# A planner's account of transfers and fillers, and the constants of its order, changed

## The chip, the cores and the metric

One core of a Trainium2 chip runs the whole program. The core has a matrix engine (TensorE, PE in the profile, with its weight loads shown apart as PEld) and three engines that work on 128 partitions side by side: VectorE (DVE), ScalarE (ACT) and GpSimd (POOL). SyncE (SP) issues the transfers. Each engine works through its own queue in order and waits at an instruction until what it needs is there. The metric is the device time of one execution in microseconds (us), as the median of some runs.

## The reference

Eight sequences of 512 rows and 128 channels pass through four layers, each of them added to its input. `ln` is a layer norm without scale.

```python
x = x + mamba(ln(x))       # W_in, short convolution, Silu, a scan over the 512 rows with 8 states
x = x + experts(ln(x))     # all 8 experts, dense, weighted by a router
x = x + attention(ln(x))   # 16 heads of 8 channels, each row sees its chunk of 10 and 25 rows before it
x = x + experts(ln(x))     # the same weights again
```

```python
g = einsum('bsh,ehf->ebsf', x, w_gate)
u = einsum('bsh,ehf->ebsf', x, w_up)
h = silu(g) * u
expert_out = einsum('ebsf,efh->ebsh', h, w_down)
out = einsum('ebsh,bse->bsh', expert_out, cw)    # cw from two softmaxes
```

The experts are most of the arithmetic: 8 experts of 128 x 512 up, 128 x 512 gate and 512 x 128 down, for 4096 rows, twice.

## The kernel before

**How the work is tiled.** A sequence's 512 rows are the columns of a tile, its 128 channels the partitions. A product of 32-bit precision is made of three passes in a rounded format (`matmul3`: high x high, low x high, high x low). So each operand is kept as a high half (a cast, mostly on ScalarE) and a low half (a subtraction, mostly on GpSimd). For one expert and one quarter of its 512 inner columns there are three products each into `g`, `u` and `y`, of 512 columns; between `u` and `y` stand Silu of `g` (ScalarE), its product with `u` (VectorE), the cast to the high half (ScalarE or VectorE) and the low half (GpSimd or VectorE). In the profile all four steps have `h` as their result. The weights are split into halves the same way as they arrive.

**What runs beside what.** The expert products of both expert layers form one stream (`ffn_stream`): layer k (0 or 1), sequence b (0 to 7), expert, quarter. Everything else is a set of generators, called lanes, that are woven into it: for each sequence a Mamba front (norm, `tp_m`, `mh`, convolution, `mde`, and the exponentials and logarithms of `mdelta`), a Mamba back (four times: `mbx`, decays `mdec`, scan `mst`, `mcc`; then `mo`), the norm and router ahead of the experts (`ffn_prep`: `tp_f`, the logits `lps_f`, `rps_f`, a softmax `pr_f`, `cps_f`), the weights of the router spread over the partitions by a transfer (`cwb`), the end of a sequence's experts (`yp`), and the attention's preparation, loads, scores (`as`), maxima (`amt`), weights (`aw`), values (`ao`) and output (`aout`).

**What sets the order.** The order of every engine's queue is fixed when the program is built, by a planner in the kernel file. `Clock` keeps an account of when each engine is free and what each operation costs (`cost`); `Engine` records every operation through one line, L269, which is why nearly all rows of the profile have that line. `Lanes.tick` chooses the lane that can start earliest; `Lanes.start` says when one can:

- Work of the experts' own chain is urgent (`hurry`) and may start up to `EDGE` early; sequence 0's first half goes with `FIRST`, its second half with `SECOND`.
- A lane whose next step is on TensorE joins the stream when its inputs have been there for `SIDE` plus a slack of `JOIN` (or the lane's own `JOIN_MAX` for the attention's maxima, `JOIN_ATT` for its preparation, `JOIN_END` for the end of the experts and of attention).
- A lane that is due is preferred by `PRESS`, and its slack is `JOIN_DUE`. Mamba is due `MAMBA_DUE` of a sequence's expert work ahead of its turn, the norm ahead of the experts `PREP_DUE`.
- While the stream itself waits, other work is held back by `HELD`.
- The softmax of the router waits until ScalarE's exponential table is loaded anyway, or until `LATE` of a sequence before it is needed.

**The first sequence** is done in two halves of 256 rows, so that the experts can begin early: `first_halves` for Mamba, then the first `SPLIT` experts on the first half, the same experts on the second half, and the rest on the whole (`passes`).

**Products of nothing.** TensorE's clock is kept up by products whose results are thrown away. Before the first expert product the planner places one (`warm`) whenever no lane can go on; its cost is that of a 256-column product plus a fixed step. Later, up to `WARM_TO` sequences, it places one (`idle`) when the stream has waited for `WARM_GAP` by the account (`keep_warm`).

**Transfers** are all issued by SyncE. In `Clock.run` the account of one is: queued behind the transfers before it, a fixed delay, its bytes at 200 KB per us, and a delay until the data can be read.

Of the kernel before, what the change touches and what calls it, by code (L numbers as in the profile page):

```python
# [87 lines left out]

TABLES = {AF.Silu: (18,), AF.Exp: (0, 6), AF.Ln: (6,), AF.Tanh: (0, 18)}
INF = float("inf")  # L90
LAGS = {"T": 0.2, "A": 0.15, "V": 0.15, "P": 0.08}
TO_PE = 0.11
SAME = 0.125
AHEAD = 0.2
EDGE = 0.1
FIRST = 0.6
LATE = 0.3
SIDE = 0.5
JOIN = 2.0
JOIN_DUE = 0.0  # L100
JOIN_MAX = 6.0
JOIN_ATT = 3.0
JOIN_END = 2.0
MOST = 6
OTHERS = 4
AT_FIRST = 7
WARM = 3.5
WARM_GAP = 0.25
WARM_TO = 1.5
SECOND = 0.2  # L110
PRESS = 0.4
HELD = 0.18
MAMBA_DUE = 0.9
PREP_DUE = 0.9
ATT_LEAD = 2.5
EARLY = 5
SPLIT = 4
EARLIEST = 2 * (DEPTH + 1)


def size(ap):

    n = 1
    for d in ap.shape[1:]:
        n *= d
    return n


class Clock:
# [96 lines left out]
    def based(self, key, base=None):  # L226
# [4 lines left out]
            [other + lag if other else 0.0]  # L231
            + [t + (LAGS[k] + lag if k != key else SAME if k in "AVP" else 0.0) for k, t in ends.items()]
        )

    def run(self, key, name, out, args, kw, after, wait):
        c = self.cost(key, name, out, args, kw)
        start = max(self.end[key] + wait, after, self.now if key == "T" else self.based(key))
        if key == "T":
            if start > self.end["T"] + 2.4:
                self.cold = start  # L240
            if start < self.cold + 3.4:
                c *= 2
        if key in "VP" and self.shares(key, name, out, args):
            start = self.with_port(start, c)
        self.end[key] = start + c
        if key == "S":
            start = max(start, self.now)
            row = out.shape[-1]
            rows = out.shape[0] * size(out) // row
            each = max(row * (2 if out.dtype == BF16 else 4), 512)  # L250
            move = rows * each / 200e3
            self.moved = max(self.moved, start + c + 0.8) + move
            return self.moved + 0.6 + move
        self.hop[key] = start + c
        return start + c + LAGS[key]

# [23 lines left out]
class Lanes:  # L280
# [29 lines left out]
    def add(self, gen, rank=1, ready=0.0, due=None, joins=None):  # L310


        self.lanes.append([gen, "", ({}, ready), rank, due, JOIN if joins is None else joins])
        self.lanes.sort(key=lambda lane: lane[3])
# [5 lines left out]
    def start(self, lane):  # L320
# [3 lines left out]
        if callable(need):  # L324
            return 0.0 if need() else INF
        if need == "T":
            if lane in self.urgent:
                return c.now if c.based("T", ready) <= c.now else INF
            wait = SIDE
            if not c.beside and not self.starved:  # L330
                wait += JOIN_DUE if lane[4] and lane[4]() else lane[5]
            return c.now if c.based("T", ready) + wait <= c.now else INF
        return min((max(c.end[key], c.based(key, ready)) for key in need), default=0.0)

    def tick(self):
# [3 lines left out]
        while True:  # L339
            c.now = max(c.now, c.end["T"])  # L340
            first, best = c.now + AHEAD, None
            for lanes in (self.urgent, self.lanes):
                for lane in lanes:
# [3 lines left out]
                    else:  # L347
                        edge = PRESS if lane[4] and lane[4]() else 0.0
                        if self.starved:
# [28 lines left out]
def block_kernel(ctx: ExitStack, tc: tile.TileContext, x, pack_a, pack_b, pack_c, w_qkv, mask, mask_t, w_o,  # L378
                 w_gate, w_up, w_down, out):
    nc = tc.nc  # L380
    clock = Clock()
# [66 lines left out]
    def load_x(b, i, tag):  # L448

        yield from lanes.take("x")  # L450
        if i:
            yield "S", done[b, i]
        t = lnp.tile([P, NT, DIM], F32, tag="x", name=f"x_{tag}", bufs=NX)
        e = sp.dma_start(out=t, in_=xs[b, i].rearrange("(t p) d -> p t d", p=P))
        return t, e
# [6 lines left out]
    def now(gen):  # L462

        try:
            next(gen)
        except StopIteration as stop:
            return stop.value
        raise AssertionError("no buffer is free")
# [30 lines left out]
    def layernorm(xc, tag, nt=NT, quick=False):  # L499
# [22 lines left out]
        for t in range(nt):  # L522
            yield "V" if quick else "AV"
            a = INF if quick else max(clock.end["A"], clock.based("A")) + 0.39
            v = max(clock.end["V"], clock.based("V")) + 0.255
# [109 lines left out]
    first = lambda gen: lanes.hurry(gen, FIRST)  # L635
    second = lambda gen: lanes.hurry(gen, SECOND)

    def mamba_front(b, sb, consts, xc):
# [25 lines left out]
        act.activation(xb[0:INNER, :], v[0:INNER, :], AF.Silu)  # L664
        there = clock.end["A"] + LAGS["A"]
        act.activation(xb[INNER:P, :], v[0:INNER, :], AF.Silu)
        there2 = clock.end["A"] + LAGS["A"]
        yield "T", there2
# [29 lines left out]
        act.activation(delta, delta, AF.Ln, bias=1.0)  # L698
        handed[b] = xb, zb, delta, bc, bc_there, clock.end["A"] + LAGS["A"]

# [322 lines left out]
    def ffn_prep(k, b, xc, t0=0, nt=NT):  # L1023
# [42 lines left out]

        yield lambda: clock.table in TABLES[AF.Exp] or pos[0] >= k * B + b - LATE
        yield "A"
# [44 lines left out]
    def ffn_finish(k, b, acc):  # L1113
        xo, there = yield from load_x(b, 2 * k + 1, f"fo{k}_{b}")
        yield "T", there
        tp = yield from side([P, NT, DIM], f"yp{k}_{b}")
        for t in range(NT):
            pe.transpose(tp[:, t, :], acc[:, t * P : (t + 1) * P], ident)
        yield "V"
        freed(dve.tensor_tensor(xo, xo, tp, ALU.add))  # L1120
        yield "S"
        store_x(b, 2 * k + 2, xo)

    def ffn_stream():
# [6 lines left out]
        def passes(k, b):  # L1131

            whole = slice(0, L)
            if k or b:
                return [(e, whole) for e in range(NE)]
            parts = [(e, slice(c * HALF, c * HALF + HALF)) for c in range(2) for e in range(SPLIT)]
            return parts + [(e, whole) for e in range(SPLIT, NE)]

        def weighted(k, b, e, cs, y, there):
# [25 lines left out]
            elif left[0] == 0:  # L1165
                lanes.add(ffn_finish(k, b, state.pop(("acc", k, b))), rank=FRANK, ready=t, joins=JOIN_END)

# [255 lines left out]
    def attention(sb):  # L1423
# [21 lines left out]
        def places(v):  # L1445
            return v.rearrange("p (i c) -> p i c", i=4)[:, :, :P].rearrange("p i (j c) -> p i j c", j=4)
# [25 lines left out]
        def load_values(s):  # L1472
# [10 lines left out]
            dve.tensor_copy(places(vtiles[s % 2])[:nk, :, :, :HD], vr[:nk])  # L1483
            v_there[s] = clock.end["V"] + LAGS["V"]

        def scores(s, both):

            qs, ks, _ = loaded[s]
            for m in range(NPAIR):
                for h in range(2):  # L1490
                    rows = slice(64 * h, 64 * h + QROWS)
                    for i, (q, k) in enumerate(blocks(steps[s][1])):
# [4 lines left out]
                        )  # L1497
            lanes.add(maxima(s, both, e), joins=JOIN_MAX)

# [101 lines left out]
        def outputs(s, o, e):  # L1601
# [11 lines left out]
            if t == len(QTILES) - 1:  # L1613
                lanes.add(joined(b, outs.pop(b)), rank=JRANK, ready=e, joins=JOIN_END)

# [103 lines left out]
    with mctx:  # L1719
        sb = msb  # L1720
        mc = {}

        def late(part):
            return lambda: pos[0] >= turn[part] - MAMBA_DUE

        def fronts(seqs):
            for b in seqs:
                turn["front"] = b
                xc = first_x
                if b:  # L1730
                    xc = yield from load_x(b, 0, f"m{b}")
                    yield lambda: ("front", b - 1) in done
                yield from mamba_front(b, sb, mc, xc)
                done["front", b] = 0.0

        def backs(seqs):
            for b in seqs:
                turn["back"] = b
                yield lambda: b in handed and (b - 1, 1) in done
                yield from mamba_back(b, sb, mc, lambda gen: lanes.add(gen, due=late("back")))  # L1740

        first(fronts(range(1)))
        first(mamba_consts(sb, mc))
        lanes.add(ffn_weights(sb))
        clock.hold = INF

        warm = now(side([P, L], "warm"))
        while (0, 0) not in ready or ready[0, 0][1] == 0:
            if lanes.tick():
                continue  # L1750
            if clock.now > WARM:
                sel = mc["sel"]
                e = pe.matmul(warm[:, :HALF], sel[:, 0], sel[:, : HALF // P], start=True, stop=True)
                clock.end["T"] += 0.1
            else:
                clock.now += 0.03
        freed(e)

        done["first"] = 0.0
        lanes.add(backs(range(1, B)), due=late("back"))  # L1760
        lanes.add(fronts(range(1, B)), due=late("front"))
        lanes.add(ffn_preps(), rank=0, due=lambda: pos[0] >= turn["prep"] - PREP_DUE)
        lanes.add(attention_preps(), rank=QRANK, joins=JOIN_ATT)
        stream = ffn_stream()

        def keep_warm():

            if pos[0] < WARM_TO and clock.now > clock.end["T"] + WARM_GAP and lanes.are_free("bank"):
                t, = take("experts", [[P, L]], ["idle"])
                sel = mc["sel"]  # L1770
                freed(pe.matmul(t[:, :HALF], sel[:, 0], sel[:, : HALF // P], start=True, stop=True), "experts")

        while "weights" not in done or (B - 1, 1) not in done:
            if next(stream):
                lanes.idle()
                keep_warm()
            else:
                lanes.tick()
# [85 lines left out]
```

## Time and profile before

| what | value |
|---|---|
| time, median of 3 runs | 1352.26 us (1350.01 to 1354.05) |
| the profiled execution | 1351.71 us, span 1349.9 us, granted TensorE clock 0.996 |
| TensorE busy | 1328.8 us, 98% of the span |
| products into u, g, y | 451.4, 448.4 and 445.6 us busy |
| GpSimd, low halves of h | 492 of 1309 ns |
| ScalarE, Silu of g and casts of h | 512 of 597 ns, 437 of 618 ns |
| VectorE, h from u | 420 of 686 ns |
| ScalarE, table loads | 125 (109 and 16 by line) of 1283 ns |

The busy times of the three kinds of expert products overlap a little, since one product begins before the one before it has left the array. The page's slices show TensorE at nine tenths or more in all but the first and the last of 40, and the chain of work that ended last lies on TensorE for 91% of the span. What the page alone doesn't show is how much of the busy time is work: fillers and products that wait inside a run are busy too.

### The profile page before, as it was taken

Reading aid. Unit: us, or ns where it says so; the run is one execution under the profiler, and the core shown is the slowest. Engines: PE = TensorE matmul, PEld = TensorE weight load, DVE = VectorE, ACT = ScalarE, POOL = GpSimd, SP = SyncE. Lnnn points to the kernel's source line nnn. Section 1 sums busy time; section 2 is a strip of 40 time slices with the busy share of each in tenths; the row PEclk is TensorE's granted clock in tenths of the full one; section 3 lists DMA queues with packets and bytes.
Section 4 is the critical chain, followed back from the end, with each engine's and each line's share of the span. In section 5 each row is a group of like instructions: output and inputs, shape, how many; then the busy total and the mean of one; then the engine's idle time right before and its main releaser. Section 6 shows DMA issues by size and latency. Waiting matters only on the chain.

```text
span 1349.9 us, 29483 instructions
## 1 busy us (share of the span) xinstructions
PE 1328.8 (98%) x10261; PEld 1053.4 (78%) x10261; DVE 1038.5 (77%) x3114; ACT 964.2 (71%) x1694; POOL 941.4 (70%) x1042
## 2 busy tenths in 40 slices
PE   7999999999999999999999999999999999999998
PEld 7877778788788877777777777777777777778886
DVE  6887888688888877897788887888888787845443
ACT  7768576867787556776777777777877767765654
POOL 5877576776767757676766767767677676777776
PEclk9999999999999999999999999999999999999999
DMA  4320303232111261344344453344443434121111
GB/s 126 95 82 28 87 24 101 64 80 76 42 48 56 63 86 52 72 102 113 79 102 114 98 125 88 95 110 102 104 99 96 114 76 102 47 71 53 40 40 40
DMA packets 182204, 107.74 MB, mean 80 GB/s; under 512 B 86401, under 2 KB 162088, under 8 KB 182056
## 3 DMA queue, kind: packets, MB, share of 16 engines
q1 hardware_dynamic: 182056, 105.87, 31.6%
q8 instruction: 81, 1.33, 0.4%
q14 instruction: 67, 0.55, 0.1%
HBM read 77.64 MB, written 27.79 MB: 78 GB/s over the span
## 4 chain that ended last, share of the span: by engine, by line
PE 91%; ACT 2%; issue 2%; POOL 2%; DVE 1%; POOLq 0%; DVEq 0%
PE u L269 26%; PE g L269 25%; PE y L269 25%; PE ao L269 2%; PE aw L269 2%; PE as L269 2%; PE mo L269 1%; POOL h L269 1%; PE aqk L269 1%; ACT h L269 1%; DVE h L269 1%; PE aout L269 1%; PE mde L269 1%; PE yp L269 1%; PE tp_f L269 0%
## 5 line engine op out<-in xcount | busy, mean ns | idle before, releaser
L269 POOL TENSOR_TENSOR h<-h,h 128x512 fp32r<-128x512 f32 x492 | 639.8, 1309 | 280.0 <-ACT h L269 223.2
L269 PE MATMUL u<-xt_f,wu 128*128 128x512 f32 (+1 forms) x1584 | 451.4, 395 | 3.6 <-ACT h L269 2.7
L269 PE MATMUL g<-xt_f,wg 128*128 128x512 f32 (+1 forms) x1584 | 448.4, 393 | 2.1 <-ACT h L269 1.9
L269 PE MATMUL y<-h,wd 128*128 128x512 f32 (+1 forms) x1584 | 445.6, 392 | 1.4 <-POOL h L269 0.8
L269 DVE TENSOR_TENSOR h<-u,h 128x512 f32<-128x512 f32 x420 | 285.8, 686 | 157.7 <-PE u L269 109.8
L269 ACT ACTIVATE h<-g 128x512 f32<-128x512 f32 x512 | 303.4, 597 | 124.8 <-PE g L269 100.6
L269 ACT CAST h<-h 128x512 fp32r<-128x512 f32 x437 | 268.3, 618 | 169.2 <-DVE h L269 167.6
L269 PEld LDWEIGHTS g<-xt_f,wg 128*128 128x128 f32 x1584 | 288.5, 189 | 70.2 <-ACT h L269 3.0
L269 PEld LDWEIGHTS y<-h,wd 128*128 128x128 f32 x1584 | 288.3, 188 | 70.3 <-POOL h L269 1.5
L269 PEld LDWEIGHTS u<-xt_f,wu 128*128 128x128 f32 x1584 | 286.7, 189 | 71.5 <-ACT h L269 4.1
L269 POOL TENSOR_TENSOR acc<-acc,cwb 128x512 f32<-128x512 f32 (+1 forms) x114 | 148.0, 1298 | 52.1 <-DVE cwb L269 44.9
L269 ACT ACT_TABLE_LOAD x109 | 139.8, 1283 | 25.2 <-PE g L269 23.7
L269 DVE CUSTOM_DVE_ANT_0 amasked<-as,maskq 128x60 f32<-128x60 f32 x640 | 95.3, 213 | 4.9 <-PE as L269 4.6
L269 DVE TENSOR_TENSOR cwb<-y,cwb 128x512 f32<-128x512 f32 (+1 forms) x116 | 77.4, 668 | 14.1 <-PE y L269 13.6
L269 DVE TENSOR_TENSOR apt<-aw,maskk 125x400 f32<-125x400 f32 (+2 forms) x160 | 88.1, 570 | 0.0
L269 DVE SCALAR_TENSOR_TENSOR h<-h,g 128x512 f32<-128x512 f32 x92 | 62.3, 681 | 28.3 <-ACT h L269 27.8
L269 ACT ACTIVATE apt<-apt 125x400 f32<-125x400 f32 (+2 forms) x160 | 81.5, 540 | 0.4
L269 DVE SCALAR_TENSOR_TENSOR h<-u,h 128x512 f32<-128x512 f32 x92 | 62.5, 683 | 3.3 <-PE g L269 0.5
L269 DVE DVE_READ_ACCUMULATOR2_ANT amx<- 128x1 f32 x640 | 51.9, 81 | 0.0
L269 DVE CAST h<-h 128x512 fp32r<-128x512 f32 x75 | 50.6, 675 | 1.2
L269 DVE COPY v<-avr 125x128 f32<-125x128 f32 (+2 forms) x40 | 25.5, 638 | 26.5 <-PE ao L269 26.0
L269 PEld LDWEIGHTS ao<-apt,v 125*32 125x32 f32 (+2 forms) x1280 | 27.4, 109 | 14.6 <-DVE h L269 4.0
(205 smaller groups left out, 1241.4 us busy)
## 6 DMA issues: line engine op xcount, KB each, us to landing
cwb<-cwd_f SPq DMA_DIRECT2D x124, 256.0 KB
aqd<-apc SPq DMA_DIRECT2D x32, 192.0 KB
ks<-aqd SPq DMA_DIRECT2D x48, 93.8 KB
x_fo<-x SPq DMA_DIRECT2D x16, 256.0 KB
aqd<-apc SPq DMA_DIRECT2D x32, 128.0 KB
x_f<-x SPq DMA_DIRECT2D x15, 256.0 KB
qs<-aqd SPq DMA_DIRECT2D x48, 75.0 KB
aod<-aos SPq DMA_DIRECT2D x24, 100.0 KB
```

The lines of the kernel that those rows point to most:

```text
L269: f(*args, **kw)
```

## The change

Two constants of the account of a transfer, the step of a filler (now named `FILL`), and the constants of the order. The code of the planner and of the computation is otherwise the same.

```diff
+FILL = 0.02
-LATE = 0.3
+LATE = 0.4
-JOIN = 2.0
+JOIN = 3.5
-JOIN_MAX = 6.0
+JOIN_MAX = 3.0
-JOIN_END = 2.0
+JOIN_END = 3.0
-WARM_GAP = 0.25
+WARM_GAP = 0.15
-SECOND = 0.2
-PRESS = 0.4
+SECOND = 0.1
+PRESS = 0.2
-MAMBA_DUE = 0.9
+MAMBA_DUE = 1.0
-SPLIT = 4
+SPLIT = 5
...
-            self.moved = max(self.moved, start + c + 0.8) + move
-            return self.moved + 0.6 + move
+            self.moved = max(self.moved, start + c + 0.6) + move
+            return self.moved + 0.8
...
                 e = pe.matmul(warm[:, :HALF], sel[:, 0], sel[:, : HALF // P], start=True, stop=True)
-                clock.end["T"] += 0.1
+                clock.end["T"] += FILL
```

Since the planner's account decides what comes next everywhere, the order of all engines' queues differs from the first filler on. The heads of TensorE's two queues (a number is how many in a row; the last numbers of a name are layer, sequence and part):

| | before | after |
|---|---|---|
| warm products up to the first `g`, in 13 runs | 111 | 161 |
| of these ahead of `mh`, of `tp_f`, of `lps_f` | 8, 23, 7 | 13, 33, 11 |
| idle products | 30 | 34 |
| experts done on the first half ahead of the second | 4 | 5 |
| table loads up to the first Silu of sequence 1, and of sequence 2 (layer 0) | 13, 19 | 7, 18 |
| table loads in all | 125 | 130 |

## The prediction

> **What bounds the kernel now.** I read the page first, then the engines' busy time by stage, then TensorE's timeline at the start, then ScalarE's in the stage where the largest late gap lies.
>
> ```profile
> PE 1328.8 (98%) x10261; PEld 1053.4 (78%) x10261; DVE 1038.5 (77%) x3114; ACT 964.2 (71%) x1694; POOL 941.4 (70%) x1042
> L269 PE MATMUL idle<-sel 128*128 128x256 f32 x30 | 8.9, 337 | 2.9 <-DVE cwt_f L269 0.9 <-ACT h L269 0.8 <-DVE mst L269 0.7
> core 0: us, PE busy (x) PEld busy (x) DVE busy (x) ACT busy (x) POOL busy (x), PEclk, DMA share, GB/s
> 34.25:59.10 24.85, 24.49 (x179) 21.64 (x179) 21.24 (x54) 16.22 (x31) 19.44 (x25) 1.00 0.32 91
> 59.10:119.30 60.20, 57.62 (x330) 47.39 (x329) 47.19 (x99) 47.53 (x85) 44.83 (x49) 0.97 0.25 72
> 119.30:213.10 93.80, 89.95 (x404) 70.39 (x403) 75.73 (x152) 65.72 (x112) 64.45 (x69) 0.98 0.18 51
> 213.10:293.90 80.80, 79.35 (x369) 63.36 (x368) 61.56 (x119) 60.08 (x102) 57.72 (x56) 1.00 0.30 82
> 293.90:371.90 78.00, 78.00 (x365) 62.11 (x364) 67.60 (x122) 58.08 (x102) 50.73 (x49) 1.00 0.22 62
> ```
>
> TensorE sets the end, but 98% busy is not 98% useful: filler products count as busy, and so do products that wait for an operand inside a run. So I count useful work instead: each product by its pace in an undisturbed run (three 512-column products in 0.70 us, six 256-column ones in 0.72, 0.11 for 128 columns), fillers at zero, and compare the sum with the clock on the wall. The expert products' places in the trace give the dates. At the first expert product (34.25 us) TensorE is 29.2 us behind its useful work; at the first product of sequence 0's second half (59.1) 36.4; where the router logits of sequence 1 are formed (118.1) 48.8; at the first product of sequence 1 (129.0) 51.1, of sequence 2 (213.1) 59.7, of sequence 3 (293.9) 64.1, of sequence 4 (371.9) 67.7. So 29 us go before the experts, 30.5 in the first two sequences, 8 in the next two. In the last stretch TensorE is busy through, and the last 80 us stand in both programs in the same order on the four compute engines. What can change is the first 300 us, where no other engine is full: VectorE's 75.73 of 93.80 is the most.
>
> ```profile
> 8.76 1.12 PE L269 MATMUL mh<-mxt,win 128*128 128x512 f32 x3
> 12.99 0.67 PE L269 MATMUL mbc<-mxb,wbc 64*128 64x256 f32 x2 [1.80 <-ACT mxb L269]
> 23.33 0.80 PE L269 MATMUL mbx<-mbc,sel 128*128 128x256 f32 x2 [2.57 <-DVE mst L269]
> 24.56 1.91 PE L269 MATMUL mo<-pa,mcx 128*128 128x128 f32 x8
> 27.54 1.05 PE L269 MATMUL mo<-pa,mcx 128*128 128x128 f32 x8
> 28.34 3.00 PE L269 MATMUL warm<-sel 128*128 128x256 f32 x23
> 31.77 0.50 PE L269 MATMUL tp_f<-ident,xn_f 128*128 128x128 f32 x2 [0.43 <-DVE xn_f L269]
> 20.00:30.00 10.00, 7.43 (x52) 7.22 (x51) 9.33 (x22) 9.28 (x20) 3.69 (x3) 0.83 0.00 0
> ```
>
> Ahead of the experts the latency of sequence 0's first half decides, and fillers (warm) sit in TensorE's queue between its steps. After the 2.57 us of idleness the granted clock falls to 0.83 over 20 to 30 us, and eight mo products take 1.91 us instead of 1.05.
>
> ```profile
> 164.71 1.28 ACT L569 ACT_TABLE_LOAD   x1
> 166.00 1.30 ACT L269 ACTIVATE mdelta<-mdelta 128x512 f32<-128x512 f32 x2
> 167.32 1.28 ACT L269 ACT_TABLE_LOAD   x1
> 168.61 1.09 ACT L269 ACTIVATE h<-g 128x512 f32<-128x512 f32 x2
> 169.72 1.28 ACT L569 ACT_TABLE_LOAD   x1
> 171.01 1.95 ACT L269 ACTIVATE mdec<-mdelta,nega 128x512 f32<-128x512 f32 x3
> 176.65 1.65 PE L269 MATMUL g<-xt_f,wg 128*128 128x512 f32 x3 [1.94 <-ACT h L269]
> ```
>
> A burst of a Mamba sequence: 11.3 us of ScalarE with four table loads and only two of the Silus (h from g) that the experts need. TensorE runs dry: 1.94 us of waiting, and products at half pace after it; 3.8 us are lost between 170 and 180 by the count above.
>
> **The change, part by part.** No kind of operation is new; the two programs differ in counts and order. Counts: 50 more warm and 4 more idle products; SPLIT makes 36 products of 512 columns into 72 of 256 (0.232 against 2 x 0.119: nothing); 5 more table loads; 5 casts, 2 weight halves and 2 reads of maxima go to VectorE, 4 halves to GpSimd; one broadcast transfer becomes two. By the rows' means that is +2.6 us on VectorE, +2.9 on ScalarE, +2.8 on GpSimd over the whole span, hidden under TensorE as long as they stay below the 84% that VectorE bears from 300 to 400 us with TensorE full.
>
> *First part, up to the first expert product.* FILL makes the build put a filler every 0.02 us of its account on top of a product's cost; a filler really steps 0.12. I walk the path. 25 fillers (23 before) ahead of tp_m and 13 (8) before mh: mh starts at 9.5 instead of 8.76, but ScalarE reads it only after its own copies end at 10.25, so 0.2 late. 10 (6) before mbx: 1.3 us into a wait of 1.1, 0.2 more; then 0.3 late. Of the 2.57 us of idleness, 14 more fillers of 0.12 in the three runs before it leave about 1.0. The 1.80 us at 12.99 left the clock at 1.00, the 2.57 did not, so I take it that 1.0 keeps it: eight mo products cost 0.9 for 1.9, the second mo no longer waits 0.8 us for TensorE, and ends 0.4 earlier. GpSimd's weight halves also end 0.7 earlier (one cast is moved ahead of the second half's decays). Then 33 fillers, 4.0 us, stand before tp_f where the data need 3.0: tp_f at 32.0 against 31.77. 11 (7) more before the logits give 0.5, the idle product ahead of the first expert product (0.42) is gone. Sum +0.2 us; if the clock drops all the same, mo pays 0.8 twice: +1.9; if the filler is covered everywhere, -0.1.
>
> The Trainium skill (TensorE: Matmul & The Clock Gate, What's actually happening) has the clock drop only after a whole idle window of some 3.4 us. Here 2.57 us were enough. By that rule the closer fillers would save nothing, and this part would be +1.0.
>
> *Second part, sequence 0 (SPLIT, MAMBA_DUE, PRESS, SECOND).* The fifth expert's half stands before the second half now, and sequence 1's Mamba back is spread behind more expert work. Useful work ahead of the second half: +4.1 us; ahead of sequence 1's logits: +8.2. What these two points wait for is the other queues. Work queued ahead of the same points: VectorE +2.3 and +3.6 (its part of the transposed input), ScalarE +2.9 and +0.8, GpSimd's variance step +3.8 and +5.3. If the queues keep the idle time they have, the point comes later by what stands in front of it, and TensorE has that much more to do meanwhile. At the logits: 8.2 - 3.6 = 4.6 won by VectorE, 2.9 by GpSimd, 7.4 by ScalarE. I take VectorE's, the fullest (47.19 and 21.24 us in the two stretches): -4.6; bounds -7.4 and 0.
>
> *Third part, sequences 1 and 2.* Sequence 2's Mamba front is put off by 20 to 30 us of TensorE work, so its burst lands behind sequence 1's first product: five table loads (5 x 1.283), softplus 1.3, decays 2.7, with two Silus, 11.6 us. That is the burst of 164.71 over again, 3.8 us; in its old place 100 to 120 us lost 2.1 and part of that stays, so +2.8. The next burst has a third Silu and casts in its middle: half of its 3.8 is left, -1.9 and 0.3 of rounding up its cover: -2.2. Sum +0.6. In all, 13 us of ScalarE and 9 of VectorE move into this stretch: 70 and 74 of some 84 us; bounds 0 and +6 (both bursts at full price with the half clock).
>
> The skill (ScalarE: Activation LUTs, What ACT_TABLE_LOAD costs) adds a drain of 1.38 us to each load. Here an ACTIVATE follows 0.01 us after it. With the drain the first burst would be 7 us longer, and this part some +5.
>
> *Fourth part, the rest.* JOIN 2.0 to 3.5 lets side products join only after more slack; JOIN_MAX cuts that of the maxima. TensorE passes between 128-row products and the narrower ones 105 times in and out instead of 108: 3 x (0.09 + 0.14) = 0.7 us saved, as the gap at each edge is in the trace. The gaps of 1.6 us at 263 and 0.9 at 521 can go or double. I take -1.0; bounds -3 and +3.
>
> *Transfers.* The account lands a 256 KB load 2.7 us after its issue instead of 4.0; in the trace the first x is issued at 0.72 and read at 3.71. No engine but SyncE waited over 1 us for a transfer after the start, so earlier reads cost nothing while landings stay near 3 us; this works only through the order, in the parts above.
>
> Sum: +0.2 - 4.6 + 0.6 - 1.0 = -4.8 us. The profiled execution took 1351.71 (span 1349.9), 0.55 below the median of 1352.26; from the median: **1347.5**.
>
> **Rivals.** *The sides wash out* (no change): GpSimd's 3.8 us ahead of the second half against 4.1 of TensorE leaves 0.3, and the rest of the second part is lost in sequence 1 again, since the same work stands ahead of sequence 2's first product in both programs (useful work differs by 0.9, VectorE's by 1.8). For it: that equality. Against: 30 us of loss with no full engine. About 1352. *The ramp empties* (more): sequence 0's 20 us of loss halve, since up to its expert 7 ScalarE has 14.7 us less in front (six table loads fewer by sequence 1's first product) and VectorE 8.3: 1351.7 - 10 - 1 = about 1341. *ScalarE's burst* (slower): it stands between sequence 1's first and fourth Silu; with PSUM banks held by products of g, TensorE stops after some 6 us. If the burst of sequence 3 behaves so too, 3.8 + 3.8 us plus two half-clock windows of 1.7, against no more than 4 us won before: +7, 1359. It decides once sequences 1 and 2 lose over 8.7 us more than now. *Fillers in the way* (the change undoes itself): +1.9 in the first part and nothing won: 1354 to 1357.
>
> **Numbers.** Forecast 0.40, ramp 0.12, wash-out 0.26, burst 0.18, fillers 0.04. 0.3% is 4.1 us, about what a measurement of this kernel tells from no change: faster (below 1348.2) 0.52, same 0.26, slower (above 1356.3) 0.22. The forecast's own range is 1343 to 1349.5; with 2 in 10 left out, 1340 to 1357.
>
> **What would show it.** After: first expert product at 34.5 +- 0.7; no low clock near 25 us, and none of the 1.91 us mo; the second half's first product near 61.5 and sequence 1's near 124 instead of 129; behind useful work at sequence 1 some 46, at sequence 2 some 56. Wrong, if tp_f comes after 33, if sequence 1 starts after 129, or if a gap over 3 us follows the table loads behind its first products.

## The result and the profile after

The changed kernel takes 1361.76 us (median of 6 runs, 1359.99 to 1363.81), the kernel before 1351.61 beside it (6 runs, 1350.01 to 1354.05): 1.0076 times as long, 95% interval 1.0062 to 1.0089. The span of the profiled execution went from 1349.9 to 1359.7 us.

The page's line of busy times:

```profile
PE 1334.8 (98%) x10351; PEld 1060.4 (78%) x10351; DVE 1044.1 (77%) x3122; ACT 965.1 (71%) x1688; POOL 942.5 (69%) x1045
```

The group of the idle products (count, busy, mean ns, idle time before them and what ended it):

```profile
L270 PE MATMUL idle<-sel 128*128 128x256 f32 x34 | 10.2, 353 | 9.1 <-ACT h L270 3.8 <-DVE mst L270 2.0 <-DVE xt_f L270 1.3
```

The engines' busy time by stage (from the first expert product to the second half, to sequence 1's first product, and to those of sequences 2, 3 and 4):

```profile
core 0: us, PE busy (x) PEld busy (x) DVE busy (x) ACT busy (x) POOL busy (x), PEclk, DMA share, GB/s
35.25:69.30 34.05, 29.97 (x219) 27.17 (x217) 28.27 (x60) 20.91 (x42) 22.15 (x28) 0.95 0.29 84
69.30:128.81 59.51, 57.30 (x357) 49.52 (x355) 46.40 (x91) 39.97 (x74) 45.87 (x48) 1.00 0.24 67
128.81:219.35 90.54, 84.62 (x376) 64.89 (x373) 68.78 (x143) 67.84 (x114) 56.07 (x63) 0.96 0.19 53
219.35:301.47 82.12, 81.14 (x377) 64.25 (x376) 68.64 (x127) 59.42 (x107) 60.66 (x59) 1.00 0.29 72
301.47:381.46 79.99, 79.80 (x379) 63.57 (x378) 65.43 (x128) 59.63 (x104) 53.75 (x52) 1.00 0.23 67
```

The share of busy time is 98% as before; it doesn't show the loss. What ends the waits ahead of the idle products does: ScalarE's `h` with 3.8 us. And the stage of sequence 1's experts (128.81 to 219.35) stands out: TensorE 5.9 us idle, clock 0.96. The prediction's count gives the same with dates. The table has how far TensorE is behind its useful work, for before in us, and for the others the difference from before; the last columns are experiments of the next section. Down to sequence 2 it is the prediction's count. That count prices attention too high, and the programs differ in how much attention stands ahead of a later date. So from sequence 4 on the differences are taken with paces fitted to the stretches where TensorE is busy through (0.233 us for 512 columns, `as` 0.010, `ao` 0.027, `aw` 0.06, `lps_f` 0.066, `mde` 0.157); at sequence 2 the two counts agree within 0.2 us. The last row is the difference of the spans. Every figure is from one profiled execution; the start alone differs by up to 3.8 us between executions of the same program (after has +1.1 at the first expert product, e8, whose program is the same up to sequence 1, +4.9).

| at | before | after | e1 | e2 | e3 | e9 | e10 | e13 | e17 |
|---|---|---|---|---|---|---|---|---|---|
| first expert product | 29.2 | +1.1 | +0.3 | +5.6 | +1.3 | +3.0 | +1.1 | +1.1 | +1.0 |
| sequence 0's second half | 36.4 | +6.1 | +2.2 | +6.7 | +5.5 | +3.0 | +5.6 | +5.7 | +5.6 |
| sequence 1, expert 0 | 51.1 | 0.0 | +1.9 | +5.9 | +4.2 | -0.2 | +0.7 | +0.8 | +0.9 |
| sequence 1, expert 1 | 51.4 | +2.4 | +1.7 | +5.7 | +5.7 | -0.3 | +2.0 | +2.0 | +3.0 |
| sequence 1, expert 2 | 51.4 | +11.3 | +9.8 | +7.9 | +9.1 | +1.8 | +4.0 | +3.9 | +7.8 |
| sequence 2 | 59.7 | +7.2 | +7.2 | +7.2 | +4.3 | +1.2 | -1.6 | -1.6 | +3.6 |
| sequence 4 | | +7.4 | +9.2 | +13.9 | +17.9 | +7.9 | +1.5 | +1.5 | +3.8 |
| sequence 6 | | +7.2 | +11.0 | +16.5 | +18.1 | +10.5 | +1.7 | +1.6 | +3.9 |
| second layer, sequence 0 | | +8.9 | +13.1 | +18.5 | +18.2 | +11.1 | +2.8 | +1.7 | +5.2 |
| end | | +9.8 | +15.2 | +21.6 | +19.3 | +13.6 | +5.5 | +1.9 | +5.3 |

So the change loses 1.1 us ahead of the experts, 5 more in sequence 0's first half, wins all of that back by sequence 1 (all but 0.8 us by the fitted paces), loses 9 in one step between sequence 1's experts 1 and 2, gets 4 of it back by sequence 2, and loses 2 to 3 more behind sequence 6.

TensorE's timeline at the start of after (start, us, what, the idle time before it):

```profile
9.38 0.86 PE L270 MATMUL mh<-mxt,win 128*128 128x512 f32 x3
...
23.51 0.50 PE L270 MATMUL mbx<-mbc,sel 128*128 128x256 f32 x2 [0.98 <-DVE mst L270]
...
25.48 1.05 PE L270 MATMUL mo<-pa,mcx 128*128 128x128 f32 x8
...
28.78 4.20 PE L270 MATMUL warm<-sel 128*128 128x256 f32 x33
32.82 0.38 PE L270 MATMUL tp_f<-ident,xn_f 128*128 128x128 f32 x2
...
38.44 0.82 PE L270 MATMUL idle<-sel 128*128 128x256 f32 x2 [1.51 <-DVE mst L270]
39.32 1.47 PE L270 MATMUL g<-xt_f,wg 128*128 128x256 f32 x6
40.58 1.91 PE L270 MATMUL mo<-pa,mcx 128*128 128x128 f32 x8
```

The idle 2.57 us ahead of `mbx` became 0.98, and no half clock (a granted clock of 0.50) follows. But the first `mo` starts at 25.48 instead of 24.56, the 33 fillers behind the second only at 28.78, and they last until `tp_f` at 32.82. And the half clock comes behind another gap, at 38.44: `g` takes 1.47 us for six products of 0.97, `mo` its 1.91.

ScalarE's timeline behind sequence 1's first products, and TensorE's in the same stretch:

```profile
138.03 1.28 ACT L270 ACT_TABLE_LOAD   x1
139.32 1.09 ACT L270 ACTIVATE h<-g 128x512 f32<-128x512 f32 x2
140.43 1.28 ACT L570 ACT_TABLE_LOAD   x1
141.72 1.95 ACT L270 ACTIVATE mdec<-mdelta,nega 128x512 f32<-128x512 f32 x3
143.71 0.72 ACT L270 ACTIVATE mdelta<-mdelta,nega 128x512 f32<-128x512 f32 x1
144.45 1.28 ACT L270 ACT_TABLE_LOAD   x1
145.74 1.57 ACT L270 ACTIVATE h<-g 128x512 f32<-128x512 f32 x3
...
142.18 0.86 PE L270 MATMUL g<-xt_f,wg 128*128 128x512 f32 x3
146.39 1.22 PE L270 MATMUL idle<-sel 128*128 128x256 f32 x2 [3.35 <-ACT h L270]
147.76 1.08 PE L270 MATMUL yp<-ident,acc 128*128 128x128 f32 x4
148.50 1.63 PE L270 MATMUL u<-xt_f,wu 128*128 128x512 f32 x3
```

Between 140.4 and 145.7 ScalarE does no Silu of an expert; TensorE runs out of things to do at 143.0, waits 3.35 us and then runs three products of `u` in 1.63 us instead of 0.86.

And VectorE's waits for transfers, in us (in total, times, longest), of after and then of before:

```profile
DVE st_a L270 <- DMA x_a<-x: 8.6, 6, 2.4
DVE st_f L270 <- DMA x_f<-x: 6.7, 3, 2.8
```

```profile
DVE st_a L269 <- DMA x_a<-x: 0.9, 1, 0.9
```

### The profile page after: what moved, and what is told of

The parts are those of the page before. It is cut to its first block, busy times and chain, and to the rows that moved or that the text cites. A ratio compares the mean times of both kernels' runs of the same rounds, so it can differ in the third digit from the quotient of the medians.

```text
span 1359.7 us, 29691 instructions
## 1 busy us (share of the span) xinstructions
PE 1334.8 (98%) x10351; PEld 1060.4 (78%) x10351; DVE 1044.1 (77%) x3122; ACT 965.1 (71%) x1688; POOL 942.5 (69%) x1045
## 4 chain that ended last, share of the span: by engine, by line
PE 88%; ACT 4%; DVE 3%; POOL 2%; issue 1%; DMA 1%; POOLq 0%; ACTq 0%; SPq 0%; DVEq 0%
PE u L270 25%; PE y L270 24%; PE g L270 24%; PE ao L270 2%; PE aw L270 2%; PE as L270 2%; ACT h L270 1%; PE mo L270 1%; ACT L270 1%; DMA x_a<-x 1%; PE aqk L270 1%; PE warm L270 1%; POOL h L270 1%; DVE h L270 1%; PE aout L270 1%
## 5 line engine op out<-in xcount | busy, mean ns | idle before, releaser
L270 ACT CAST h<-h 128x512 fp32r<-128x512 f32 x432 | 265.1, 618 | 176.3 <-DVE h L270 175.0
L270 DVE TENSOR_TENSOR cwb<-y,cwb 128x512 f32<-128x512 f32 (+1 forms) x117 | 77.4, 663 | 13.5 <-PE y L270 13.1
```

Source lines behind the costliest of these rows:

```text
L270: f(*args, **kw)
```

## The experiments

Each ran beside the kernel before, on the same chip as it.

| run | median us | before us | ratio, 95% interval |
|---|---|---|---|
| e1 account only | 1369.16 | 1352.18 | 1.0123 (1.0108 to 1.0138) |
| e2 fillers only | 1373.45 | 1352.18 | 1.0153 (1.0138 to 1.0168) |
| e3 constants only | 1372.60 | 1352.18 | 1.0147 (1.0122 to 1.0171) |
| e4 after, no idle products | 1358.46 | 1352.18 | 1.0048 (1.0033 to 1.0063) |
| e5 before, SIDE 0.52 | 1353.14 | 1351.89 | 1.0009 (1.0000 to 1.0018) |
| e6 before, lag 0.155 | 1356.00 | 1351.89 | 1.0035 (1.0022 to 1.0048) |
| e7 before, EDGE 0.11 | 1354.59 | 1351.89 | 1.0026 (1.0015 to 1.0037) |
| e8 after, burst without loads | 1363.04 | 1351.89 | 1.0082 (1.0065 to 1.0099) |
| e9 before, held | 1365.69 | 1351.68 | 1.0103 (1.0086 to 1.0119) |
| e10 after, pulled | 1358.61 | 1351.68 | 1.0050 (1.0031 to 1.0069) |
| e11 e10, no idle products | 1359.82 | 1351.68 | 1.0056 (1.0035 to 1.0077) |
| e12 before, no idle products | 1351.69 | 1351.68 | 0.9998 (0.9988 to 1.0008) |
| e13 e10, old account late | 1354.12 | 1351.75 | 1.0025 (1.0014 to 1.0037) |
| e14 before, new account late | 1354.00 | 1351.75 | 1.0022 (1.0011 to 1.0033) |
| e15 before, lag late | 1351.12 | 1351.75 | 1.0002 (0.9993 to 1.0011) |
| e16 e10, measured landing | 1379.23 | 1351.75 | 1.0213 (1.0198 to 1.0228) |
| e17 e8 without clips | 1357.12 | 1351.39 | 1.0047 (1.0034 to 1.0060) |
| e18 mixed | 1361.29 | 1351.39 | 1.0064 (1.0049 to 1.0079) |

**The parts alone (e1, e2, e3), and the idle products out (e4).** e1 is before with the two lines of the account; e2 is before with `FILL = 0.02`, `WARM_GAP = 0.15`; e3 has all other constants of the change, with the old account and fillers. e4 leaves the idle products out of the program but not out of the account:

```diff
-                freed(pe.matmul(t[:, :HALF], sel[:, 0], sel[:, : HALF // P], start=True, stop=True), "experts")
+                freed(clock.run("T", "matmul", two, (two, sel[:, 0], two), {}, 0.0, 0.0), "experts")
```

> The kernel before with only the account of transfers changed. Theory C (the account lands transfers too early, and VectorE stands at norms whose rows have not come: 15.3 us of such waits in the changed kernel against 0.9): 1357 to 1361 us, with over 5 us of VectorE waiting for x_f and x_a. Theory A (the loss is the second Mamba sequence's burst on ScalarE, put off by the order's constants to behind sequence 1's first products) and theory B (fillers that wait for a PSUM bank hold up the products behind them): within 3 us of the kernel before, and no gap over 3 us on TensorE between 130 and 160 us.

> The kernel before with only FILL 0.02 and WARM_GAP 0.15. Theory B: 1355 to 1360 us, with idle products waiting over 15 us in all (8.6 before, 21 in the changed kernel). Theories A and C: within 3 us of the kernel before. Under all three the first expert product comes near 35 us instead of 34.3, since 33 fillers stand ahead of the transposes where the data need fewer.

> The changed kernel with the old account of transfers, FILL 0.1 and WARM_GAP 0.25; all the other constants new. Theory A: 1357 to 1362 us, with a gap over 3 us behind the table loads of the second Mamba sequence. Theories B and C: within 3 us of the kernel before.

> The changed kernel in the same order on every engine, without the 34 idle products ahead of the second sequence's experts and without the PSUM bank each takes; the planner still books their time. They feed nothing. Theory B: 1352 to 1357 us, the gaps at 36.7, 142.6 and 154.0 us shrink by over half. Theory A: 1358 to 1362, the gap at 142.6 stays over 2.5 us since the products behind it wait for the same Silu. Theory C: no change, 1360 to 1363.

Each part alone loses 17 to 21 us, the three together 10. So the loss isn't a sum of the parts, and no part is to blame alone. All three came out above every range that was expected of them. e4 is 3.3 us faster than after, in the range of theory A; the step at sequence 1 stays (+6.8 us behind before at expert 2, from -0.4 at expert 1).

**Is any new order worse (e5, e6, e7)?** Three changes of before that stand for nothing.

```diff
-SIDE = 0.5
+SIDE = 0.52
...
-LAGS = {"T": 0.2, "A": 0.15, "V": 0.15, "P": 0.08}
+LAGS = {"T": 0.2, "A": 0.155, "V": 0.155, "P": 0.08}
...
-EDGE = 0.1
+EDGE = 0.11
```

> The kernel before with SIDE 0.52 for 0.5, a number that stands for nothing measured; the order differs from the first product of sequence 3's experts in the second layer's numbering of side products on (the program agrees up to there). Theory 'selected order': the order of before is one good draw, and any new draw loses; 1356 to 1372. Rival 'meaning': the constants cost by what they say, and 0.02 us more patience costs nothing; 1350 to 1355.

> The kernel before with the account's lag of ScalarE and VectorE 0.155 for 0.15 us; the order parts in sequence 0's second half of experts, at expert 3. Theory 'selected order': 1356 to 1372, with the losses at places that have nothing to do with one another. Rival 'meaning': 5 ns of an estimate cost nothing; 1350 to 1355.

> The kernel before with EDGE 0.11 for 0.1; the order parts near sequence 0's expert 4 in its fourth quarter. Theory 'selected order': 1356 to 1372. Rival 'meaning': 1350 to 1355.

They cost 1.3, 4.1 and 2.7 us: e5 and e7 lie in the rival's range, e6 at the lower edge of the theory's. A new order costs a little more often than not, but neither 10 nor 17 to 21.

**What the bad ones share.** By useful TensorE work ahead of it, the product `mh` of sequence 2's Mamba front stands at 47.1 us in before and in e5 to e7, and `mde` at 56.2: in sequence 0's second half. In after they stand at 73.6 and 78.4, in e1 at 65.9 and 73.5, in e2 at 66.5 and 72.7, in e3 at 76.5 and 77.6, where sequence 1's first product stands at 78. So in all four sequence 2's front comes 19 to 29 us of TensorE work late, with its exponentials, decays and scans close around sequence 1's first products. Two kernels try that place alone: e9 is before with the front held back, e10 after with it pulled forward.

```diff
                     xc = yield from load_x(b, 0, f"m{b}")
                     yield lambda: ("front", b - 1) in done
+                    if b == 2:
+                        yield lambda: pos[0] >= 0.7
```

```diff
-        lanes.add(fronts(range(1, B)), due=late("front"))
+        lanes.add(fronts(range(1, B)), due=lambda: turn["front"] == 2 and pos[0] >= 0.6 or late("front")())
```

> The kernel before with one line more: sequence 2's Mamba front may not start before sequence 0's experts are 0.7 done (its products mh stand at 66.6 us of useful TensorE work instead of 47.1, mde at 72.8 instead of 56.2; after has 73.6 and 78.4; sequence 1's experts start at 78). Constants and account are those of before. Theory 'place of sequence 2's Mamba': that place alone is what after and the three part-changes have in common; nothing changes before 80 us, 7 to 10 us are lost at sequence 1's experts 1 and 2 as in after, some of it comes back, and the end is 1357 to 1364. Rival 'sum of small things' (the constants lose where they act, the place is a by-product): 1351 to 1355.

> The changed kernel with its constants, account and fillers, but sequence 2's Mamba front counts as due from 0.6 of sequence 0's experts on (mh at 51.1 us of useful work, mde at 56.2, where before has it). Theory 'place': the step of +9.0 at sequence 1's expert 2 falls to between 0 and +3, sequence 2 starts at +0 to +3 against before instead of +7.2, and with the 1.1 us of the head and the 2 to 3 us of the second layer's start the end is 1351 to 1356. Rival 'sum of small things': 1359 to 1364.

e10: the step at expert 2 is 2.0 instead of 9.0 us, sequence 2 starts at -1.6 instead of +7.2, and the second layer at +2.8 instead of +8.9. The windows of sequence 1's expert 0 and expert 1, in after and then in e10:

```profile
128.81:140.78 11.97, 11.46 (x54) 8.16 (x51) 7.30 (x21) 11.03 (x19) 5.09 (x9) 1.00 0.04 10
140.78:159.24 18.46, 14.20 (x52) 10.07 (x50) 15.89 (x27) 11.56 (x19) 8.27 (x9) 0.82 0.18 52
```

```profile
130.51:141.06 10.55, 10.43 (x45) 7.52 (x44) 10.55 (x19) 9.38 (x17) 8.37 (x13) 1.00 0.00 0
141.06:153.91 12.85, 12.77 (x65) 10.22 (x64) 11.64 (x20) 5.90 (x12) 9.06 (x8) 1.00 0.28 85
```

In after ScalarE is busy for 11.03 of the first 11.97 us and VectorE for 15.89 of the 18.46 behind them; TensorE stands idle for 4.3 us and runs at 0.82: of the step some 3 us are the half clock, 6.83 us long, behind that idle time. In e10 ScalarE has only 5.90 of 12.85 there, TensorE idles 0.1 us, and its clock is 1.00. Pulling the front redraws the order behind it too, but no redrawn order of e5 to e7 moves the time by 9 us. The whole is only 3.1 us faster than after, between the two expected ranges: 3.8 us go behind sequence 6, where after loses 2.6.

e9 is a miss in its place and a hit in its sum: 14 us slower from that one line, above the range, but only 2 of them at sequence 1's expert 2; 9 go in sequences 2 to 5 (+1.2 to +10.5), and 3 behind. Its later fronts are late as well (sequence 3's `mh` at 123.5 us of useful work instead of 83.7; 123.4 in e2). So one late front puts off all that come after it. Where that is paid depends on the rest: at once in after, e1 and e3 (steps of 8.9, 8.1 and 3.4 us at expert 2, the last behind 1.5 at expert 1), later and more in e2 and e9, which have both the old account and the old constants of the order. The two largest steps, of after and e1, hold 6.83 us of half clock each; those of e2, e3 and e9 hold none.

**How the late front costs 9 us (e8, e17).** e8 issues Silu instead of Exp and Ln for sequence 2 and leaves out the three table loads that go with them, in after's order; e17 also leaves out that sequence's four clips. So both leave out what sequence 2's decays mean, and only their times are read.

```diff
-        table("natural_log_exp_and_others", 6)
-        act.activation(delta, delta, AF.Exp)
-        act.activation(delta, delta, AF.Ln, bias=1.0)
+        swap = AF.Silu if b == 2 else None
+        table("natural_log_exp_and_others", 6, b != 2)
+        act.activation(delta, delta, AF.Exp, swap=swap)
+        act.activation(delta, delta, AF.Ln, bias=1.0, swap=swap)
...
-                decs["t", i] = act.activation(decs[i], delta, AF.Exp, scale=nega[:, i : i + 1])
+                decs["t", i] = act.activation(decs[i], delta, AF.Exp, scale=nega[:, i : i + 1], swap=AF.Silu if b == 2 else None)
...
-                decs["c", i] = dve.tensor_scalar(decs[i], decs[i], cap[:, i : i + 1], 1e-4, ALU.min, ALU.max)
+                decs["c", i] = dve.tensor_scalar(decs[i], decs[i], cap[:, i : i + 1], 1e-4, ALU.min, ALU.max, skip=b == 2)
```

> The changed kernel with its order kept on all engines, but sequence 2's softplus and decays computed with Silu in place of Exp and Ln, which leaves out their meaning and three of the five table loads of the burst behind sequence 1's first product (3 x 1.283 = 3.85 us less on ScalarE there). Theory 'ScalarE's burst': sequence 1's step of +9.0 at its expert 2 falls to about +5, the gap over 3 us ahead of the idle products goes below 1, and sequence 2 starts about 4 us sooner; 1357 to 1358.5. Rival 'something else waits there' (VectorE's wait for x behind its decays): the step stays within 1 us, 1361 +- 1. Rival 'made up later': the step falls, and the end stays at 1361 +- 1.

> The kernel of e8 (the changed kernel, sequence 2's softplus and decays as Silu, three table loads fewer), and sequence 2's four clips of decays on VectorE left out too (1.88 + 0.47 + 0.46 = 2.8 us of VectorE between 143 and 149 us in after); the order of the rest is kept. Theory 'ScalarE first, VectorE next': in e8 the loss moved from the wait for h to the wait for sequence 3's normalised x, whose statistics stand behind these clips on VectorE; without them the step at sequence 1's expert 2 falls from 9 to 11 us to 2 to 6, and the end to 1356 to 1359. Rival 'neither': the step stays over 8, 1360 to 1364.

In e8 the step at expert 2 is 8.7 us (from +4.6 to +13.3), so 3.85 us less on ScalarE bring almost nothing there. The gap of 3.35 us is gone, but others came. Its timeline on VectorE, GpSimd, ScalarE and TensorE:

```profile
144.65 1.89 DVE L270 TENSOR_SCALAR mdec<-mdec,cap 128x512 f32<-128x512 f32 x2
146.47 0.37 DVE L270 BATCH_NORM_AGGREGATE mv_m<-st_m 128x2 f32<-128x6 f32 x4
...
147.20 1.02 POOL L270 TENSOR_TENSOR rs_m<-va_m,half_power 128x4 f32<-128x4 f32 x1
...
148.81 0.88 ACT L270 ACTIVATE xn_m<-x_m,nm_m,rs_m 128x128 f32<-128x128 f32 x2 [1.92 <-POOL nm_m L270]
...
151.17 0.86 PE L270 MATMUL tp_m<-ident,xn_m 128*128 128x128 f32 x2 [1.10 <-ACT xn_m L270]
```

The two clips hold VectorE until 146.5, so the statistics of sequence 3's Mamba norm (`mv_m`) are late, so GpSimd's and ScalarE's steps of that norm, so TensorE's `tp_m`, which stands in front of expert products; behind it TensorE runs at half clock for 6.83 us from 151.26. In e17, with the clips gone, `mv_m` no longer stands behind them, the same gap of 1.10 us ahead of the second `tp_m` is still there, but no half clock follows, the step is 4.8 us, and the whole is 4.6 us faster than after:

```profile
148.86 0.71 PE L271 MATMUL tp_m<-ident,xn_m 128*128 128x128 f32 x2 [1.10 <-ACT xn_m L271]
149.33 0.94 PE L271 MATMUL g<-xt_f,wg 128*128 128x512 f32 x3
```

The windows from sequence 1's expert 1 to its expert 2, in e8 and then in e17:

```profile
143.03:161.15 18.12, 15.39 (x51) 9.96 (x49) 15.84 (x27) 8.52 (x16) 8.17 (x9) 0.81 0.20 56
141.40:155.68 14.28, 12.34 (x51) 8.24 (x49) 12.66 (x21) 7.80 (x15) 7.99 (x9) 1.00 0.25 69
```

e17's step is half of after's, but most of what it wins over e8 is the clock: 6.83 us of half clock are 3.4 of the 3.8 us between the two windows. Without the clips the second `tp_m` comes only 0.7 us sooner, counted from the same products ahead of it. What the two edits take away is idle time of TensorE: 4.3 us in after, 2.7 without the loads, 1.9 without the clips too, against 0.1 in e10. So ScalarE's loads and VectorE's clips each have a part of some 1 us in it. That VectorE decides once ScalarE's part is gone isn't shown, since the half clock depends on how the gaps fall in its windows as well (last section). The granted clocks of the other runs (0.996 in all four of e8, 0.997 to 0.999 in e17) say that e8 had more half clock in each of them, but not why. What makes the remaining 1.9 us was not tried.

**The idle products again (e11, e12).** The edit of e4, in e10 and in before.

> The kernel of e10 without its idle products (fillers between expert products) and the PSUM banks that they take; the order of the rest is that of e10. The idle products took 3.3 us in after: 3 us under e10, 1348 to 1353. Rival 'they keep the clock up': 1 to 4 us over e10.

> The kernel before without its 30 idle products and the banks that they take; the order of the rest is kept. By the same price 30/34 x 3.3 = 2.9 us: 1348 to 1350. Rival 'they keep the clock up': 1352 to 1356.

e12: 1351.69 against 1351.68 us, so in before the idle products cost nothing and keep nothing up. e11 is 1.2 us slower than e10, which its interval doesn't tell from nothing. The 3.3 us of e4 hold for after's order alone.

**The second layer (e13 to e16).** What differs there: VectorE waits for reads of `x`. e13 is e10 with the old account from the first layer's sequence 6 on, e14 before with the new one there, e15 before with 5 ns of lag there, e16 e10 with a landing of 5.9 us there. The programs are the same up to that point.

```diff
+                        clock.far = pos[0] >= 6.0
...
-            self.moved = max(self.moved, start + c + 0.6) + move
-            return self.moved + 0.8
+            if self.far:
+                self.moved = max(self.moved, start + c + 0.8) + move
+                return self.moved + 0.6 + move
+            else:
+                self.moved = max(self.moved, start + c + 0.6) + move
+                return self.moved + 0.8
```

> The kernel of e10, with the account of transfers of before from the first layer's sequence 6 on (the order is the same up to there). Theory 'account': VectorE's waits for x fall from 10 us to under 4, the 4.6 us lost between the second layer's start and the end go to 0 to 1.5, and the time falls from 1358.6 to 1353 to 1355.5. Rival 'redrawn order': the waits fall, the loss stays between 2 and 5 us, 1356 to 1360.

> The kernel before, with the new account from the first layer's sequence 6 on (same order up to there). Theory 'account': VectorE waits 7 us or more for x, 3.5 to 5 us lost, 1355 to 1357. Rival 'redrawn order': anything from 1350 to 1356, as e15.

> The kernel before, with 5 ns more lag for ScalarE and VectorE in the account from the first layer's sequence 6 on: a new draw of the order there with no meaning. Theory 'account': 1351 to 1353, no loss there. Rival 'redrawn order' (the order of before is a lucky one there): 2 to 5 us lost behind the second layer's start as in e5 and e6, 1354 to 1357.

> The kernel of e10, with the landing of a read put at 5.9 us after its issue for 256 KB from the first layer's sequence 6 on, as the traces have it for the reads of x there. Theory 'account': VectorE's waits for x go below 2 us and the loss to 0 to 1.5 us, 1353 to 1355.5, no worse than e13. Rival 'redrawn order': 1356 to 1360.

e13 is 4.5 us faster than e10; from sequence 6, where the two part, to the end it loses 0.3 us instead of 3.8, and VectorE's waits for `x_a` are gone. (The 4.6 us of the expectations come from the count that prices attention too high.) e14 is 2.2 us slower than before, under its range, e15 as fast as before. So the switch back is worth 4.5 us in e10. That the account as such costs there is not shown: from sequence 6 on e14 loses 1.5 us in its profiled execution, e5 and e6, changes without a meaning, 2.6 and 2.3, and e15 0.5. Nor is a wait of VectorE for `x` a loss by itself: e15 has 4.9 us of waits for `x_a` (five, the longest 1.8) and is as fast as before. In after's timeline one such read:

```profile
829.58 2.14 SPq L270 DMA_DIRECT2D x_a<-x  x1
...
835.93 0.49 DVE L270 BATCH_NORM_STATS2 st_a<-x_a 128x6 f32<-128x128 f32 x2 [2.40 <-DMA x_a<-x]
```

It is read 6.35 us after its issue, 2.40 of them spent waiting; the issue alone took SyncE 2.14 us. The six reads of `x_a` between 570 and 1000 us were read 5.9 to 6.4 us after their issue. The new account has 2.7 us behind the issue, so VectorE's statistics are queued too early, and what stands behind them waits too. e16 is the largest miss: with 5.9 us in the account the time is 1379.23 us, and 25 us are lost from the first layer's sequence 7 on; the clock is at half for 10 us from 703 on and again from 887 on. The edit puts 3.2 us more on the landing of every transfer, not of the reads of `x` alone. The account is also what decides when work becomes due, and a figure that is true of one kind of read, put on all transfers, was not the best one.

**e18.** e10 up to sequence 2, then before's account and constants, and one filler of four left out late in the head (its edit is those of e13 and of each constant, switched by `clock.far`).

> The kernel of e10 up to sequence 2, then the account and the constants of before, and one filler of four left out behind 24 us of the build's clock (14 fillers, 8 of them ahead of tp_f). If the parts add: 8 x 0.12 = 1 us in the head, e10's -1.6 us at sequence 2 kept, and no loss behind: 1348.5 to 1351, at or just under before. Rival 'a new order behind sequence 2 costs its own 2 to 6 us', as e5 to e7: 1352 to 1357.

10 us slower than before (its runs lie between 1356.97 and 1362.28): +3.3 us already at the first expert product, with half clock from 28.4 on for 3.41 us, +5.7 at sequence 1, and 4.6 more behind. Whether the fewer fillers did that or the start's own scatter was not separated, and what the new order behind sequence 2 costs stays open with it. No version here beats before.

## Why the prediction was wrong

**Sum.** Forecast -4.8 us, measured +9.8 in the span. By its parts, as differences of the count: first part +1.1 (forecast +0.2), second -1.1 (-4.6), third +7.2 (+0.6), fourth with the transfers +2.6 (-1.0).

**First part.** Its mechanism was right: `mbx`'s wait fell to 0.98 us, no half clock near 25, `mo` at 1.05 and 1.16 us. The 33 fillers took their 4.0 us, but began at 28.78, where the walk had 28.0, because the first `mo` came 0.9 late, and the second ended 0.4 later than in before where the walk had 0.4 earlier; so `tp_f` came at 32.82 and the first expert product at 35.25, just out of 34.5 +- 0.7. A loss it can't be called: in eight executions with before's head (before, e5 to e7, e9, e12, e14, e15) the first expert product stands at 0 to 3.0 us on this scale, five of them at 2.3 or more. Not foreseen: the half clock moved behind a gap of 1.51 us at 38.44.

**Second part.** "If the queues keep the idle time they have" failed. The second half came at 69.3 instead of 61.5, and sequence 1 at 128.8 instead of 124: of the 4.6 us 1.1 are left. The choice of VectorE as the fullest doesn't fit the shown row either: from 59.10 to 119.30 ScalarE has 47.53 us, VectorE 47.19. In after sequence 0 loses 5 us between its first product and its second half, 1.7 of them in a stretch of 3.41 us at half clock; and without the idle products sequence 1 starts 3.4 us earlier (e4: -3.4).

**Third part.** This is the step that decided: the late burst of sequence 2 was seen, and priced by the burst at 164.71 at +2.8, since the same loads cost 3.8 us there. It cost 9.0 at once and 7.2 up to sequence 2, more than the bound of +6. The price was wrong because it was that of one burst on ScalarE with one wait behind it: at 176 us before had a wait of 1.94 us and 3.41 us of half clock, and in after the step has 4.3 us of idle time and 6.83 of half clock. e8 shows that three loads fewer take only 1.5 us of the idle time, since `tp_m` of sequence 3's norm waits instead, and leave the half clock; e17 that 1.9 us stay idle without the clips too, with no half clock behind; e10 that all but 2.0 us of the step go away with the place. So the place is shown as the cause; how the loss divides between the engines is not. The skill's drain of 1.38 us per load (ScalarE: Activation LUTs, What ACT_TABLE_LOAD costs), which would have made this part +5, isn't in the rows of after either: an ACTIVATE starts 0.01 us behind each load.

**Fourth part and transfers.** "No engine but SyncE waited over 1 us for a transfer after the start, so earlier reads cost nothing while landings stay near 3 us" failed: 3 us is the landing of a lone read, those of attention took 5.9 to 6.4, and VectorE's waits for `x` went from 0.9 to 15.3 us. e13 gives 4.5 us back, e14 costs 2.2; but e15's waits of 4.9 us cost nothing, so the account's share of the 2.6 us stays open.

**Rivals.** ScalarE's burst (1359) was nearest to the time and named the right place. Its threshold of 8.7 us lost in sequences 1 and 2 wasn't reached (7.1), its end was, with 2.6 us more lost behind sequence 2; and e8 shows that ScalarE's loads alone aren't the mechanism. "Fillers in the way" had a part: +1.1 in the head, and 3.3 in e4. The wash-out and the emptied ramp are out. Of the conditions named for being wrong, the gap of over 3 us behind the table loads came true (3.35); `tp_f` after 33 and sequence 1 after 129 were missed by 0.2 us each.

**What stays open.** Why each of three unlike parts tips sequence 2's front out of sequence 0's second half; only that they do, and what it costs, was shown. How much of the step each engine brings, and when two windows of half clock follow. And the 1.9 us by which e13's span is still longer than before's.

## What to carry to other kernels

Where a planner fixes the order, look first for the one piece of work whose place flips, and try that place alone with one condition, before pricing the parts: three parts that cost 17 to 21 us each and 10 together can't be summed. A late burst must be priced on every engine it loads, with the half clock behind it, since taking the first wait away brought up another here (e8). A constant of an account is tuned together with its other constants; one that is "nearer the trace" for a lone transfer (2.7 us for 3.0) was further from it for a read among those of attention (5.9 to 6.4).

## What the runs showed of the hardware

The half clock follows half-empty windows rather than long gaps. Each stretch of half clock in the traces is 3.41 us long, or a multiple, on a fixed grid (in before 23.03, 70.82 and 176.63: 14 and 31 steps apart). Busy time and clock in the window before a drop and in the dropped one, twice in after:

```profile
36.15:39.56 3.41, 1.79 (x11) 1.19 (x10) 3.37 (x7) 0.60 (x1) 1.35 (x2) 1.00 0.70 208
39.56:42.97 3.41, 3.41 (x16) 3.07 (x16) 2.81 (x9) 0.60 (x1) 0.00 (x0) 0.50 0.03 13
141.97:145.38 3.41, 1.07 (x5) 0.54 (x3) 3.41 (x9) 3.36 (x5) 2.43 (x2) 1.00 0.56 180
145.38:152.21 6.83, 5.61 (x15) 4.28 (x16) 5.08 (x9) 4.62 (x10) 4.30 (x6) 0.50 0.00 0
```

Over the 20 traces of this study (windows up to 1200 us on each trace's own grid, at full clock before): of 19 windows with TensorE busy under 0.47 of the time, 18 were followed by half clock; of 40 between 0.47 and 0.58, 16; of 102 up to 0.75, 11; of 6,777 above that none. So the same gap of 1.10 us has half clock behind it in e8, where its window is 0.58 busy, and none in e17, where it is 0.68: what else is in the window counts, and with it where the grid falls, which differs from execution to execution (with the same head the drop is at 39.56 us in after and 40.08 in e4). Between 0.47 and 0.75 the share alone doesn't settle it. The Trainium skill (TensorE: Matmul & The Clock Gate, What's actually happening) has a free-running window of 3413 ns, which agrees; its "idle window" need not be idle: here the windows were 0.52 and 0.31 busy. That also mends the prediction's reading that a gap of 2.57 us was "enough" and one of 1.80 was not: in before the window behind which the clock fell was 0.33 busy, the one with the gap of 1.80 us 0.53.
